# Layer 2 of a four-layer fp32 kernel: one context product a sequence, smaller steps between the score products, and a later start of the recurrence

## The chip, the cores and the metric

The kernel runs on one core of a Trainium2 chip. The metric is the device time of one execution in microseconds (us). The profile is that of another, single execution of the same program. Engines are written as the profile does: PE is TensorE (PEld its weight loads), DVE is VectorE, ACT is ScalarE, POOL is GpSimd, SP is SyncE.

## The reference

The program applies four layers to an activation x of 8 sequences of 512 positions and 128 features. Each layer does `x = x + s * silu(f)`, where s is a mixer and f a feed-forward part, both computed from the layer-normalised x. The change is inside layer 2. Its two parts are, cut to what matters:

```python
# s: _L2_attn_ref, 16 heads of 8 features, causal
qkv = ln(x) @ qkv_w + qkv_b
scores = q @ k.T / sqrt(8), future positions masked
attn = softmax(scores) @ v @ out_w + out_b
x = x + attn
ctx = attn
xs, vs = ln(x), 0
for _ in range(8):                                  # the recurrence
    u = tanh(ctx @ w_ctx + xs @ w_x + b_inl)        # ctx @ w_ctx is the same each time
    vs = vs + 0.1 * (u - xs - vs)
    xs = xs + 0.1 * vs
x = x + xs
s = x + gelu(ln(x) @ ff_w1 + ff_b1) @ ff_w2 + ff_b2
# f: _L2_ffn_ref, 128 -> 512 -> 512 -> 512 -> 128
h = silu(x @ w1 * w1_s) * (x @ w2 * w2_s)
h = gelu(h @ h1 * h1_s)
h = gelu(h @ h2 * h2_s)
f = h @ w3 * w3_s
```

## The kernel before

Everything is fp32. Layers 0, 1 and 3 stay as they are. Layer 2 works a sequence at a time; a sequence (b from 0 to 7) is a tile of 128 partitions by 512 columns, in either orientation. The 16 heads are four groups (g) of four heads, each head in a strip of 32 partitions. A *unit* is one sequence, one group and one block of 128 keys (kc from 0 to 3), so a sequence has 16 units and the layer 128. For a unit:

- `weights` computes transposed scores of the four heads into two PSUM tiles `pu` (two banks each), 512, 384, 256 or 128 columns wide as kc grows (L1390), then ACT takes the Exp (L1422) and POOL clears the future positions (L199).
- `maxima` computes, some units ahead, the scores in the other orientation (L1390) with an additive mask (L1401), also into two `pu` tiles, and DVE reduces them to the row maximum (L1404) in the tile `mpad`. `put_maxima` transposes `mpad` on PE (L1411) and adds it to the queries (L1412), in a row where the keys hold -1, so that the maximum is subtracted by the product itself.
- `sums` multiplies the weights of the unit LAG = 2 before with the values (L1435), into the bank `pf`; after the last key block the result is copied out (L120 on ACT and L122 on DVE in turn) as `oT`.

[...] two `pu` tiles of two, one `pf`, and three `pa` for all other products.

Other work is written as generators whose `yield`s cut it into steps. `begin(b)` normalises, transposes and makes queries, keys and values. `ffn(b)` computes f: four steps of w1 and w2 (L1359, L1360), then h1 and h2, each one step of sixteen products of 512 columns (L1372) with four Gelus (L1373), then w3 (L1379). `group(b, g)` transposes the sums back (L1449), divides, and after the last group makes the attention's output and the context `ctx` (L1463 to L1468). `rest(b)` normalises, runs the eight iterations of the recurrence (w_ctx L1485, w_x L1486, Tanh L1488, update L1490 to L1493), normalises again, and runs the last two products (L1509, L1515) and the way into x (L1523 to L1527).

The PE order is written out by hand: PE runs instructions just as the Python code issues them. The other engines' orders are made by a scheduler from the same program. The main loop issues, for each unit u: `weights(u)`; a step of the queue `back` (group and rest); `put_maxima` at the end of a group; a step of the queue `front` (begin and ffn of the next sequence); `maxima(u + 5)`; one more step of `back` or `front`, in turn; `sums(u - 2)`. Before the loop, the five first maxima and then all of `ffn(0)` run; after it, what is left in `back` runs alone, namely the last group and the whole `rest(7)`. A pass in what follows is one product of 128 by 128 with 512 columns, which the trace shows as two instructions.

Of the kernel before, what the change touches and what calls it, by code (L numbers as in the profile page):

```python
# [20 lines left out]
P = 128  # L21
B = 8
# [1158 lines left out]
def pack2(i):  # L1181
# [10 lines left out]
    p.add("own", one)  # L1192
    bq, bk = (strips2(b[None, n * C : (n + 1) * C]).reshape(2, P).T for n in range(2))
# [4 lines left out]
    bk[16::32] = -1.0  # L1198
    p.add("bk", bk)
# [58 lines left out]
class Layer2(BySequence):  # L1258
# [39 lines left out]
    def begin(self, b):  # L1298

        k, nc, cn, tp = self.k, self.k.nc, self.cn, self.tp  # L1300
# [13 lines left out]
        yield  # L1314
        q["xT"] = tp.tile([P, T], F32, name="xT2", bufs=1)
        k.to_features(xn, q["xT"], nt=JT)
        yield
# [4 lines left out]
        yield  # L1322
        q["qT"] = tp.tile([P, 4, T], F32, name="qT2")
        q["kT"] = tp.tile([P, 2, T], F32, name="kT2")
        for t in range(2):
# [13 lines left out]
            yield  # L1339
# [8 lines left out]
        yield  # L1348

    def ffn(self, b):  # L1350
# [5 lines left out]
        for o in range(4):  # L1356
# [8 lines left out]
            yield  # L1365
        for n in ("h1", "h2"):
            src, hA = hA, hid()
            for o in range(4):
                ps = k.pa()
                for i in range(4):  # L1370
                    c0 = i * FF2 + o * P
                    nc.tensor.matmul(ps, fn[n][:, c0 : c0 + P], src[:, i, :], start=(i == 0), stop=(i == 3))  # L1372
                nc.scalar.activation(hA[:, o, :], ps, AF.Gelu, scale=fn[n + "_s"][:, o : o + 1])  # L1373
            yield
        f = q["f"] = tp.tile([P, JT, C], F32, name="f2", bufs=3)
        ps = k.pa((P, JT, C))
        for j in range(JT):
            for i in range(4):
                nc.tensor.matmul(  # L1379
                    ps[:, j, :], hA[:, i, j * P : (j + 1) * P], fn["w3"][:, i * C : (i + 1) * C],  # L1380
                    start=(i == 0), stop=(i == 3),
                )
        nc.vector.tensor_tensor(f, ps, bc(fn["w3_s"], 1, JT), ALU.mult)
        yield
# [7 lines left out]
    def maxima(self, b, g, qt):  # L1392
        k, nc, q = self.k, self.k.nc, self.q[b]
        qT, kT = q["qT"][:, g, :], q["kT"][:, g // 2, :]
# [7 lines left out]
        for i, pu in pairs:  # L1402
            top = self.mpad[g % 2][:, qt, :].rearrange("p (i c) -> p i c", c=32)
            nc.vector.tensor_reduce(top[:, i : i + 2, 16], pu[:, :, 0:m], AX.X, ALU.max)  # L1404

    def put_maxima(self, b, g):

        k, nc, qT = self.k, self.k.nc, self.q[b]["qT"][:, g, :]
        ps = k.pa((P, JT, P))
        for t in range(JT):  # L1410
            nc.tensor.transpose(ps[:, t, :], self.mpad[g % 2][:, t, :], k.ident)  # L1411
        nc.vector.tensor_tensor(qT, qT, ps.rearrange("p a b -> p (a b)"), ALU.add)  # L1412
# [30 lines left out]
    def group(self, b, g):  # L1443
# [11 lines left out]
        yield  # L1455
# [4 lines left out]
        yield  # L1460
# [6 lines left out]
        q["ctx"] = tp.tile([P, T], F32, name="ctx2")  # L1467
# [677 lines left out]
```

## Time and profile before

| | |
|---|---|
| three runs | 3640.08, 3640.95 (median), 3649.79 us |
| profiled execution: its time, its span | 3647.2 us, 3645.5 us |
| mean granted clock of PE | 0.83 of full speed |
| layer 2, from its first maxima to its last product | 1477.5 to about 2628 us of the span |
| PE instructions of L1390, L1435, L1372, L1485, L1486 | 2048, 1024, 512, 128, 128 |
| ACT_TABLE_LOADs of layer 2 | 29 of 1.28 us each |
| PE, DVE, ACT busy over the span | 77%, 64%, 45% |

The profile names instructions by the line of the kernel, and tiles by their names in the program. A wait is put down to the engine that came last. Busy PE is modelled, so the starts of instructions tell more than their ends. The granted clock is a share of full speed; in layer 2 it is either 1.0 or 0.5 for stretches of 3.4 us.

### The profile page before, as it was taken

The page shows a single profiled execution, that of the slowest core. Times are in us where ns is not written, and L with a number is a line of the kernel's source. Part 1 is how long each engine was busy: PE and PEld are TensorE (multiplying, and loading weights), DVE is VectorE, ACT ScalarE, POOL GpSimd, SP SyncE. Part 2 cuts the span into 40 slices and gives each one's busy share as a digit, 9 for nine tenths or more (in the row PEclk, how much of TensorE's full clock was granted, in tenths as well). Part 3 has the DMA queues.
Part 4 walks back from the last instruction along what each step waited for, and adds up shares of the span by engine and source line. Part 5 has one row for each costly group of instructions (what it writes and reads, how often), then busy time and mean ns, then how long its engine had stood idle before and what let it go on. Part 6 is the DMA issues. An engine that isn't in the chain of part 4 may idle for free.

```text
span 3645.5 us, 44996 instructions
## 1 busy us (share of the span) xinstructions
PE 2815.7 (77%) x16390; PEld 1512.3 (41%) x16390; DVE 2315.1 (64%) x6346; ACT 1645.2 (45%) x3211; POOL 743.0 (20%) x845
## 2 busy tenths in 40 slices
PE   6173657512998897799999999999678789887987
PEld 4142445302444454344444444443344445444543
DVE  7989898997582334334544544444467777777775
ACT  5162546512544445233333333333245566665665
POOL 0004040400225553101101101101121222222221
PEclk9585757555789999799999999998868889888988
DMA  4003030311002222000000000000000000000000
GB/s 119 2 2 71 1 82 1 72 48 34 1 2 50 41 39 41 42 1 1 1 1 1 1 1 1 1 1 1 21 1 1 4 4 1 4 3 4 1 4 7
DMA packets 67519, 64.53 MB, mean 18 GB/s; under 512 B 5344, under 2 KB 59616, under 8 KB 66784
## 3 DMA queue, kind: packets, MB, share of 16 engines
q1 hardware_dynamic: 39264, 42.75, 3.8%
q0 software_dynamic: 19712, 14.69, 3.1%
q10 hardware_dynamic: 8320, 4.19, 0.4%
q8 instruction: 129, 2.11, 0.2%
q14 instruction: 94, 0.77, 0.1%
HBM read 43.80 MB, written 17.83 MB: 17 GB/s over the span
## 4 chain that ended last, share of the span: by engine, by line
PE 36%; DVE 17%; ACT 7%; POOL 3%; issue 2%; DMA 1%; POOLq 0%; ACTq 0%; DVEq 0%; SPq 0%
PE pa L1372 6%; PE pu L1390 6%; DVE nm L1960 4%; ACT at L1961 3%; PE pu L1957 3%; PE pf L1942 2%; DVE mpad L1404 2%; PE pf L1435 2%; PE pa L1486 1%; PE pa L1485 1%; PE pa L1870 1%; ACT at L1422 1%; PE pa L1915 1%; DVE rope L1863 1%; PE pa L1509 1%
## 5 line engine op out<-in xcount | busy, mean ns | idle before, releaser
L1961 ACT ACTIVATE at<-pu,nm 128x512 f32<-128x512 f32 x512 | 348.1, 688 | 151.6 <-DVE nm L1960 125.1
L1960 DVE TENSOR_REDUCE nm<-pu 128x1 f32<-128x512 f32 x512 | 326.8, 680 | 66.6 <-PE pu L1957 66.5
L199 POOL TENSOR_SCALAR_AFFINE_SELECT at<-at 128x512 f32<-128x512 f32 x184 | 123.3, 670 | 1004.3 <-ACT at L1422 855.9
L1404 DVE TENSOR_REDUCE mpad<-pu 128x2 f32<-128x256 f32 (+3 forms) x256 | 199.2, 818 | 168.6 <-PE pu L1401 168.6
L1422 ACT ACTIVATE at<-pu 128x1024 f32<-128x1024 f32 (+3 forms) x256 | 171.7, 702 | 285.7 <-PE pu L1390 285.5
L1078 ACT ACTIVATE at<-pu,rsqrt 128x1024 f32<-128x1024 f32 (+3 forms) x256 | 190.9, 793 | 190.1 <-PE pu L1073 164.4
L1957 PE MATMUL pu<-qT,kT 32*128 32x512 f32 x1024 | 246.4, 703 | 6.0 <-ACT at L1961 5.1
L1372 PE MATMUL pa<-hid,f 128*128 128x512 f32 x512 | 222.7, 593 | 0.0
L1390 PE MATMUL pu<-qT,kT 32*128 32x512 f32 (+3 forms) x1024 | 160.8, 516 | 56.4 <-DVE mpad L1404 42.0
L748 PE MATMUL pa<-ident,Y 128*128 128x128 f32 x32 | 7.9, 426 | 210.9 <-DVE Y L739 210.9
L1390 PE MATMUL pu<-kT,qT 32*128 32x128 f32 (+3 forms) x1024 | 151.8, 569 | 14.4 <-ACT at L1422 10.2
L1942 PE MATMUL pf<-at,va 128*32 128x512 f32 x1024 | 158.9, 698 | 1.4 <-POOL va L1935 1.4
L548 POOL DMA_INDIRECT xg<-xn_d,idx x48 | 54.9, 1143 | 496.9 <-PE pf L552 316.3
L1372 PEld LDWEIGHTS pa<-hid,f 128*128 128x128 f32 x512 | 96.6, 190 | 119.5 <-issue 118.9
L1493 DVE SCALAR_TENSOR_TENSOR X<-X,u 128x512 f32<-128x512 f32 x56 | 38.7, 691 | 159.5 <-ACT u L1488 159.5
L1073 PE MATMUL pu<-qT,kT 32*128 32x512 f32 (+3 forms) x1024 | 131.1, 518 | 5.7 <-ACT at L1078 4.7
L1390 PEld LDWEIGHTS pu<-qT,kT 32*128 32x128 f32 x1024 | 67.5, 197 | 155.5 <-DVE mpad L1404 116.3
L1016 POOL DMA_INDIRECT f_d<-ys,idx x64 | 103.6, 1619 | 138.0 <-DMA f_d<-ys,idx 86.0
L1935 POOL TENSOR_TENSOR va<-V,sm 128x32 f32<-128x32 f32 x128 | 38.8, 303 | 451.7 <-DVE sm L1934 401.5
L1957 PEld LDWEIGHTS pu<-qT,kT 32*128 32x128 f32 x1024 | 81.9, 209 | 103.2 <-ACT at L1961 65.5
L1373 ACT ACTIVATE hid<-pa,f 128x512 f32<-128x512 f32 x64 | 44.0, 688 | 172.5 <-PE pa L1372 172.5
L1083 DVE TENSOR_TENSOR at<-at,ceiling 128x512 f32<-128x512 f32 x72 | 50.2, 698 | 108.2 <-ACT at L1078 104.8
(611 smaller groups left out, 6723.3 us busy)
## 6 DMA issues: line engine op xcount, KB each, us to landing
w<-in_w_dram SPq DMA_DIRECT2D x24, 512.0 KB, 3.8
f_d<-zeros ACTq DMA_DIRECT2D x8, 512.0 KB
xn_d<-xn SPq DMA_DIRECT2D x8, 512.0 KB, 4.9
w<-in_w_dram SPq DMA_DIRECT2D x16, 256.0 KB, 2.9
w<-in_w_dram SPq DMA_DIRECT2D x24, 128.0 KB
f<-in_f_dram SPq DMA_DIRECT2D x1, 2888.0 KB, 11.8
xn<-in_x_dram SPq DMA_DIRECT2D x4, 512.0 KB, 9.3
Gt<-in_x_dram SPq DMA_DIRECT2D x4, 512.0 KB
```

The lines of the kernel that those rows point to most:

```text
L199: self.nc.gpsimd.affine_select(a, a if src is None else src, pattern, ALU.is_ge, 0.0, base=0, channel_multiplier=-1)
L1016: nc.gpsimd.indirect_dma_start(out=self.f_d, out_offset=bass.IndirectOffsetOnAxis(ap=idx[:, e, i : i + 1], axis=0), in_=ys[:, i, :], in_of ...
L1073: nc.tensor.matmul(pu[:, n, 0:m], q["kT"][r, g // 2, kc * P : kc * P + P], q["qT"][r, g, kc * P :], start=True, stop=True,)
L1078: nc.scalar.activation(at_[:, i : i + 2, 0:m], pu[:, :, 0:m], AF.Square, bias=k.rsqrt2, scale=32.0**-0.5)
L1372: nc.tensor.matmul(ps, fn[n][:, c0 : c0 + P], src[:, i, :], start=(i == 0), stop=(i == 3))
L1390: self.k.nc.tensor.matmul(pu[:, n, 0:m], a[r, c0 : c0 + P], b[r, q0 : q0 + m], start=True, stop=stop)
L1404: nc.vector.tensor_reduce(top[:, i : i + 2, 16], pu[:, :, 0:m], AX.X, ALU.max)
L1422: nc.scalar.activation(at_[:, i : i + 2, 0:m], pu[:, :, 0:m], AF.Exp, scale=8.0**-0.5)
L1942: nc.tensor.matmul(po[i * 32 : i * 32 + 32, :], va[:, kc, c0 : c0 + 32], E[:, i, :], start=(kc == 0), stop=(kc == JT - 1))
L1957: nc.tensor.matmul(pu, q["kT"][r, kc * P : (kc + 1) * P], q["qT"][r, g, :], start=True, stop=True)
L1960: nc.vector.tensor_reduce(nm[:, w], pu, AX.X, ALU.max, negate=True)
L1961: nc.scalar.activation(E[:, n, :], pu, AF.Exp, bias=nm[:, w], accum_out=sm[:, w])
```

## The change

All of it is in layer 2:

- `w_ctx @ ctx` is computed once a sequence in `group`, copied to SBUF by ACT, and added by DVE to each iteration's product before the Tanh.
- The maxima of two groups of heads lie side by side in one `mpad` (columns 16 and 17 of a strip); `put_maxima` transposes once for both and adds each to its own queries with a mask `put`. The keys hold -1 in both rows. Maxima run 9 units ahead in place of 5.
- h1 and h2 are cut into steps of two passes, with a PSUM bank `ph` of their own (one buffer), and `pa` has two buffers in place of three. w3 and ff_w2 are cut in two halves, ff_w1 too.
- Each `yield` says how many passes its step holds. The loop gives out shares of passes: one after the weights, one after the maxima; the wider the scores just issued, the larger the share. `group` goes ahead of `rest`, `rest` ahead of `front`; one step of group or rest a share, and as many of `front` as the credit allows.
- `begin(b + 1)` is put ahead of what is left of `ffn`, at the end of a sequence's second unit; the first `ffn` is woven with the first nine maxima.

The diff, cut to its core (unchanged parts of `begin`, the assertions and the constants left out):

```diff
     def ffn(self, b):
...
         for n in ("h1", "h2"):
             src, hA = hA, hid()
             for o in range(4):
-                ps = k.pa()
+                ps = k.psum("ph", (P, T))
                 for i in range(4):
+                    if i == 2:
+                        yield 2.0
                     c0 = i * FF2 + o * P
                     nc.tensor.matmul(ps, fn[n][:, c0 : c0 + P], src[:, i, :], start=(i == 0), stop=(i == 3))
                 nc.scalar.activation(hA[:, o, :], ps, AF.Gelu, scale=fn[n + "_s"][:, o : o + 1])
-            yield
+                yield 2.0
...
     def maxima(self, b, g, qt):
...
-            top = self.mpad[g % 2][:, qt, :].rearrange("p (i c) -> p i c", c=32)
-            nc.vector.tensor_reduce(top[:, i : i + 2, 16], pu[:, :, 0:m], AX.X, ALU.max)
+            top = self.mpad[g // 2][:, qt, :].rearrange("p (i c) -> p i c", c=32)
+            nc.vector.tensor_reduce(top[:, i : i + 2, 16 + g % 2], pu[:, :, 0:m], AX.X, ALU.max)
-    def put_maxima(self, b, g):
+    def put_maxima(self, b, t):
-        k, nc, qT = self.k, self.k.nc, self.q[b]["qT"][:, g, :]
+        k, nc, qT, put = self.k, self.k.nc, self.q[b]["qT"], self.cn["put"]
         ps = k.pa((P, JT, P))
-        for t in range(JT):
-            nc.tensor.transpose(ps[:, t, :], self.mpad[g % 2][:, t, :], k.ident)
-        nc.vector.tensor_tensor(qT, qT, ps.rearrange("p a b -> p (a b)"), ALU.add)
+        for qt in range(JT):
+            nc.tensor.transpose(ps[:, qt, :], self.mpad[t][:, qt, :], k.ident)
+        top = ps.rearrange("p a b -> p (a b)")
+        for v in range(2):
+            to = qT[:, 2 * t + v, :]
+            nc.vector.scalar_tensor_tensor(to, top, put[:, v : v + 1], to, ALU.mult, ALU.add)
...
     def group(self, b, g):
...
-        q["ctx"] = tp.tile([P, T], F32, name="ctx2")
-        nc.scalar.activation(q["ctx"], ps, AF.Identity, bias=self.out_bc, scale=100.0)
-        yield
+        ctx = tp.tile([P, T], F32, name="ctx2", bufs=1)
+        nc.scalar.activation(ctx, ps, AF.Identity, bias=self.out_bc, scale=100.0)
+        yield 2.25
+        ps = k.pa()
+        nc.tensor.matmul(ps, cn["w_ctx"], ctx, start=True, stop=True)
+        q["ctx"] = tp.tile([P, T], F32, name="cw2")
+        nc.scalar.copy(q["ctx"], ps)
+        yield 1.0
...
     def rest(self, b):
...
         self.layernorm(xn, h)
-        yield
-        yield
+        yield 0.0
         k.to_features(h, X[0], nt=JT, scale=self.g1[:, 0:1], bias=self.g1[:, 1:2])
-        yield
+        yield 1.25
         for it in range(ITERS):
             now, then = X[it % 2], X[1 - it % 2]
             ps = k.pa()
-            nc.tensor.matmul(ps, cn["w_ctx"], q["ctx"], start=True, stop=False)
-            nc.tensor.matmul(ps, cn["w_x"], now, start=False, stop=True)
+            nc.tensor.matmul(ps, cn["w_x"], now, start=True, stop=True)
             u = tp.tile([P, T], F32, name="u2")
-            nc.scalar.activation(u, ps, AF.Tanh, bias=cn["b_inl"], scale=0.01)
+            nc.vector.tensor_tensor(u, ps, q["ctx"], ALU.add)
+            nc.scalar.activation(u, u, AF.Tanh, bias=cn["b_inl"], scale=0.01)
...
-            yield
+            yield 1.0
...
 def layer2(k, x, A, at):
...
-        ctx.enter_context(k.banks("l2p", pu=2, pf=1, pa=3))
+        ctx.enter_context(k.banks("l2p", pu=2, pf=1, pa=2, ph=1))
...
-        AHEAD = JT + 1
-        for u in range(AHEAD):
-            L.maxima(*units[u])
-        for _ in L.ffn(0):
-            pass
-        L.put_maxima(0, 0)
         U = 4 * JT
-        front = back = iter(())
+        PAIR = 2 * JT
+        AHEAD = PAIR + 1
+        def maxima(u):
+            b, g, n = units[u]
+            L.maxima(b, g, (n - 1) % JT)
+        first = L.ffn(0)
+        for u in range(AHEAD):
+            maxima(u)
+            next(first, None)
+        L.put_maxima(0, 0)
+        for _ in first:
+            pass
+        front = groups = rest = iter(())
+        credit = 0.0
+        def fill(u, second):
+            nonlocal credit
+            wide = 1.5 - u % JT
+            share = (2.4 + 0.6 * wide, 2.4 - 0.6 * wide)[second] if u >= U else 1.8
+            share += 0.3 - 0.6 * second
+            passes = next(groups, None)
+            if passes is None:
+                passes = 0.0 if second and u % 2 == 0 else next(rest, 0.0)
+            credit = min(credit, share) + share - passes
+            while credit > 0.0:
+                passes = next(front, None)
+                if passes is None:
+                    break
+                credit -= passes
         for u in range(len(units) + LAG):
             b, n = divmod(u, U)
             if u < len(units):
                 held[u] = L.weights(*units[u])
-            next(back, None)
-            if n == 1 and b + 1 < B:
-                front = chain(L.begin(b + 1), L.ffn(b + 1))
-            if u % JT == JT - 1 and u + 1 < len(units):
-                L.put_maxima(*units[u + 1][0:2])
-            next(front, None)
+                if u % PAIR == PAIR - 1 and u + 1 < len(units):
+                    L.put_maxima(units[u + 1][0], units[u + 1][1] // 2)
+            fill(u, False)
             if u + AHEAD < len(units):
-                L.maxima(*units[u + AHEAD])
-            next(back if u % 2 else front, None)
+                maxima(u + AHEAD)
+            fill(u, True)
             if u >= LAG:
                 wb, g, kc = units[u - LAG]
                 L.sums(wb, g, kc, held.pop(u - LAG))
                 if kc == JT - 1:
-                    back = chain(L.group(wb, g), back)
+                    groups = chain(groups, L.group(wb, g))
                     if g == 3:
-                        back = chain(back, L.rest(wb))
-        for _ in back:
-            pass
+                        rest = chain(rest, L.rest(wb))
+            if n == LAG - 1 and b + 1 < B:
+                front = chain(L.begin(b + 1), front, L.ffn(b + 1))
+        for _ in chain(groups, rest):
+            next(front, None)
```

## The prediction

> **What bounds the kernel now.** I read the page first, then the busy time by stretches of layer 2, the waits of TensorE, the groups of instructions by line and form, and at last the timeline of a few places.
>
> ```profile
> PE 2815.7 (77%) x16390; PEld 1512.3 (41%) x16390; DVE 2315.1 (64%) x6346; ACT 1645.2 (45%) x3211; POOL 743.0 (20%) x845
> ```
>
> TensorE (PE) is the busiest engine. The change touches only layer 2, so I cut that layer at the first instruction of each sequence's first weights. The columns are: stretch, its length, busy PE, PEld, DVE, ACT, POOL, granted clock, DMA.
>
> ```profile
> 1477.50:1533.30 55.80, 50.85 (x179) 25.05 (x179) 15.33 (x24) 10.82 (x14) 0.00 (x0) 0.88 0.00 0
> 1533.30:1648.90 115.60, 105.79 (x598) 47.78 (x598) 39.95 (x58) 36.25 (x52) 11.41 (x17) 0.91 0.00 1
> 1648.90:1782.50 133.60, 125.16 (x686) 57.34 (x682) 60.17 (x94) 48.18 (x70) 14.57 (x20) 0.95 0.00 1
> ...
> 1919.60:2058.70 139.10, 130.74 (x719) 61.52 (x716) 65.19 (x105) 50.25 (x72) 18.31 (x23) 0.93 0.00 1
> ...
> 2472.20:2560.00 87.80, 78.85 (x498) 34.81 (x494) 43.42 (x68) 31.52 (x49) 13.18 (x18) 0.86 0.00 1
> 2560.00:2634.10 74.10, 44.32 (x170) 22.62 (x170) 28.99 (x50) 15.41 (x22) 9.58 (x12) 0.84 0.07 26
> ```
>
> These are the prologue, sequence 0, sequence 1, one of the five steady sequences (137.1 to 139.1 us), sequence 7, and the way out of sequence 7. PE is 94% busy in a steady sequence, but at clock 0.93, so about 14% of the time runs at half speed. ACT is at 36% and DVE at 47%: neither is a bound. The chain of waits over layer 2 names PE lines first, then DVE mpad L1404 (6.0%) and ACT at L1422 (3.3%). PE's own waits in this stretch are nearly all for a score bank:
>
> ```profile
> PE pu L1390 <- DVE mpad L1404: 45.9, 73, 1.7
> PE pu L1390 <- ACT at L1422: 23.2, 45, 1.4
> ```
>
> **What a sequence needs of PE.** From starts in the timeline: a pass (512 columns, two instructions) takes 0.86 us, 0.91 where the line changes; four heads' scores of 512, 384, 256, 128 columns take 1.07, 0.86, 0.65, 0.43; their sums 0.95, 0.78, 0.57, 0.36; four transposes 0.49; a mask 0.23. All work of one sequence comes to 111 us at full clock. A steady sequence takes 138, so 27 are lost. Two causes can be counted. Between weights and maxima the Exps must free the banks, between maxima and the next weights the reductions must:
>
> ```profile
> L1404 DVE TENSOR_REDUCE mpad<-pu 128x2 f32<-128x1024 f32 x64 | 75.4, 1220 | 39.8 <-PE pu L1401 39.8
> L1422 ACT ACTIVATE at<-pu 128x1024 f32<-128x1024 f32 x64 | 61.9, 1019 | 33.2 <-PE pu L1390 33.1
> ...
> L1422 ACT ACT_TABLE_LOAD x14 | 18.0, 1283 | 12.7 <-PE pu L1390 12.7
> ```
>
> Two of these in a row plus 0.2 us: 2.2 us of cover wanted after 512-wide weights, 2.6 after 512-wide maxima, less for the narrower (rows of the other forms: 808, 598, 384 and 951, 684, 418 ns). Laid along PE's order, what other work covers falls short by 15.6 us a sequence. The halved clock accounts for up to 10 more (18 us at half speed). That leaves 2: so the two causes explain the loss.
>
> **The change, part by part.** One execution carries the sum: 3647.2 us (span 3645.5), which lies 6.2 above the median of the three runs, 3640.95; my differences are put on the median.
>
> 1. *Context's product once.* L1485 goes from 16 to 2 instructions a sequence: 7 products of 0.97 us, 6.8 us of PE; its ACT copy costs 0.58 (row L120 COPY) with ACT idle. But u now needs a DVE addition of 0.69 us before the Tanh. In place of product, Tanh, update it is product, addition, Tanh, update, and the context product no longer fills PE meanwhile.
>
> 2. *Maxima in pairs of groups.* Two sets of transposes fewer, 1.0 us of PE; DVE keeps four additions (0.69 each, now with a scalar, nearest row 0.69 to 0.75), in pairs: the score of the next group waits 0.7 longer behind the pair, covered by 512-wide maxima (1.3). AHEAD 9 in place of 5 moves four maxima (3.5 us of PE) from the tail into the prologue.
>
> 3. *Steps of at most 2.5 passes, shared by width.* This is the gain aimed at. In the order of the changed kernel the 13.9-us blocks of L1372 are spread over the units, and the shortfall after maxima falls from 9.1 to 0.5 us a sequence. Shares also fall short of need: a sequence's shares come to 76.8 passes less 30.3 for groups and rest, 46.5, while begin and ffn want 52.75. Some 5 us of PE work a sequence is put off, so sequences 1 to 6 hold 99.5 us of PE work (111 less 7.8, plus 1 for more line changes, less 5), and sequence 7, which had 67, holds 89.
>
> 4. *The table loads.* Gelu now stands alone between Exps. The instruction order has 133 table loads in layer 2 where it had 29: 104 more, 13 a sequence. The trace's row says 1283 ns, so 133 us of ACT. The Trainium skill speaks against exactly this, in ScalarE: Activation LUTs, section "Table sets: the hidden batching unit": calls should be batched by table set. Its example puts about 2.7 us on a load; by that the 104 would be 281 us, an estimate from that page. The row decides: 1.28. ACT rises from 50 to 67 us a sequence, still no bound. But 67 of the loads stand before an Exp and wait with it for PE, so they lengthen the path by which banks come free from 2.2 to 3.5 us; the shortfall after weights rises from 6.5 to about 10.
>
> 5. *Banks.* ph has one buffer, pa two where it had three. A pa bank is free only after its reader; ahead of that reader on DVE stand two reductions (2.4 us), on ACT two Exps (2.0) and perhaps a load. A ph bank waits for a Gelu (0.69) behind a load (1.28). Who waits is PE, with all that is queued behind. The trace has no stall at a third pa bank; bounds: 0, and the whole queue, 3 us each.
>
> 6. *POOL and SP* keep 755 and 90 rows in both kernels' instruction orders: the causal masks, bias additions and x's addition move with their steps; no transfer is moved past another; the constants grow by two columns. I cost this at nothing: POOL, 13% busy in a steady sequence, hides it, and sums come two units after their weights, some 13 us; without that cover each mask would cost its 0.64 us (row L199).
>
> To price 3 to 5 together I followed the sixteen units of one steady sequence along the orders of PE, ACT and DVE with the durations above. PE lost: 6.2 us on Exps behind loads, 4.1 on sums' copies queued behind a Gelu or an update, 2.2 on the recurrence, 7.1 on pa banks, 2.3 on ph, 1.1 on reductions, and some 2 because PE's result reaches a reader 0.25 us after the last column. Sum 25: a steady sequence of 99.5 + 25 = 124.5 at full clock.
>
> **The clock.** The trace shows when it halves:
>
> ```profile
> 1901.10:1904.50 3.40, 1.85 (x20) 0.68 (x16) 3.37 (x8) 0.95 (x3) 1.34 (x2) 1.00 0.00 0
> 1904.50:1907.90 3.40, 3.03 (x11) 1.67 (x12) 2.27 (x5) 1.48 (x3) 1.40 (x2) 0.51 0.01 2
> ```
>
> A stretch of 3.4 us in which PE was busy 54% is followed by half clock (at 1925.0, 62%), with no gap over 1.7 us in it. The skill's TensorE: Matmul & The Clock Gate, section "Why this matters for your kernels", asks only that no gap exceed about 3 us; by that rule the changed kernel would stay at full clock, and a sequence take 124.5. By the rows, stalls of 1.4 to 2.0 us (about six places in the sequence I followed) each halve the clock for two stretches or so, 41 us; PE would lose some 14 us in them and get 5 or 6 back where later stalls vanish: 133. I take the rows.
>
> **The sum.** Sequences 1 to 6: 6 x 133 = 798 against 823.3 (the stretch rows added), -25. Sequence 0: 83 us of work, 21.5 of shortfall, 7 of bank waits, 6 of clock, 118 against 115.6, +2. Sequence 7: 89 of work, 23 of stalls (recurrence steps now stand next to each other), 6 of clock, 118 against 87.8, +30. Prologue: 3.9 us of maxima more and five ph waits of 0.95, less about 4 because PE warms up earlier, 61 against 55.8, +5. The way out: the eight iterations run alone there.
>
> ```profile
> 2590.94 1.12 PE L1486 MATMUL pa<-X,c 128*128 128x512 f32 x2
> ...
> 2592.11 0.69 ACT L1488 ACTIVATE u<-pa,c 128x512 f32<-128x512 f32 x1 [1.94 <-PE pa L1486]
> 2592.83 0.69 DVE L1493 SCALAR_TENSOR_TENSOR X<-X,u 128x512 f32<-128x512 f32 x1 [1.14 <-ACT u L1488]
> ...
> 2593.57 1.12 PE L1486 MATMUL pa<-X,c 128*128 128x512 f32 x2 [0.65 <-DVE X L1493]
> ```
>
> One takes 2.63; L1485 was hidden in it and kept PE warm. With the addition 3.36, and with PE busy a quarter of the time half clock is likely, 4.15: +11 (between 6 and 12). Total: -25 +2 +30 +5 +11 = +23 us.
>
> **Rivals.**
> *The clock holds* (the page's rule): steady sequences of 124.5, -76, the rest +48: -28, 3613 us. For it: PE work is spread evenly. Against: the rows above.
> *Only the widths' shortfall remains* (110 + 5 a sequence): sequences 1 to 6 at 690, sequence 7 at 100, sequence 0 at 106: about -120, 3520 us. For it: before, this count came within 2 us. Against: before had three pa banks and 4 Gelu visits a sequence.
> *ACT's loads lengthen every path more than I counted*, steady sequences of 142: +77, 3718 us. It decides from 129 on: there the six sequences' gain, 49, equals what prologue, sequences 0 and 7 and way out cost, 48.
> That the change doesn't do what it says: L1485's products are once a sequence in the order, so this is out.
>
> **How the numbers follow.** Forecast (133 a sequence, 3664 us): 0.54, its own spread 127.5 to 138; of it 0.08 lie within 0.3% (11 us, about what a measurement of this kernel can tell from no change). Clock holds: 0.27, of which 0.20 faster and 0.07 same. Widths only: 0.07, faster. Loads: 0.12, slower. So faster 0.27, same 0.15, slower 0.58. The range 3590 to 3722 leaves out the widths-only case and the far ends of the others.
>
> **What would show it.** Right: 133 table loads; steady sequences near 133 with clock under 0.92; PE waits on pa, ph and L1467; iterations over 3.3 us in the way out; sequence 7 near 118. Wrong: sequences under 125 with clock near 1, or DVE or ACT over 80% busy.

## The result, and the profile after

Twenty executions of each kernel: 3639.22 us after (3631.48 to 3645.72), 3645.24 before (3633.87 to 3662.48); the ratio is 0.9978, with a 95% interval of 0.9969 to 0.9988. The change made the kernel faster by 0.22%, where the forecast was 0.63% slower. The profiled execution has a span of 3638.0 us, 7.5 less than the one of before.

The page's line of the engines, first:

```profile
PE 2745.3 (75%) x16214; PEld 1453.1 (40%) x16214; DVE 2359.3 (65%) x6426; ACT 1780.1 (49%) x3323; POOL 746.6 (21%) x845
```

PE lost 70 us of busy time, and the span 7.5. So the question is where the rest went: in layer 2 PE is busy 62 us less (1058.4 to 996.7) and idle 59 us more. Here is the busy time by stretches of layer 2, cut at each sequence's first weights (length; busy PE, PEld, DVE, ACT, POOL; clock; DMA): the prologue, sequences 0, 1 and 3, sequence 7 up to its last sums, and the way out behind them.

```profile
1480.20:1536.40 56.20, 51.88 (x226) 23.64 (x225) 23.26 (x32) 10.82 (x14) 0.00 (x0) 1.00 0.00 1
1536.40:1646.90 110.50, 102.22 (x574) 43.31 (x573) 40.66 (x59) 52.44 (x65) 11.24 (x17) 0.92 0.00 1
1646.90:1782.00 135.10, 117.83 (x656) 51.62 (x652) 66.10 (x104) 61.99 (x81) 14.83 (x20) 0.92 0.00 1
...
1912.60:2043.10 130.50, 116.14 (x688) 51.63 (x684) 70.52 (x116) 61.74 (x81) 18.40 (x23) 0.96 0.00 1
...
2440.90:2556.80 115.90, 99.59 (x568) 45.01 (x564) 47.59 (x78) 65.70 (x82) 14.88 (x20) 0.96 0.00 1
2556.80:2628.50 71.70, 35.78 (x105) 15.10 (x104) 30.17 (x50) 11.54 (x17) 6.95 (x7) 0.61 0.03 8
```

The prediction ended sequence 7 of before with its last weights (87.8 us). Cut at the last sums, as here, the same two stretches of before are:

```profile
2472.40:2573.50 101.10, 88.93 (x550) 40.91 (x553) 45.35 (x70) 35.49 (x52) 14.80 (x20) 0.86 0.00 1
2573.50:2630.60 57.10, 34.03 (x119) 16.34 (x118) 24.75 (x41) 10.78 (x16) 6.80 (x7) 0.85 0.04 12
```

Against the forecast, the differences to before:

| stretch | forecast us | measured us |
|---|---|---|
| sequences 1 to 6 (794.0 against 823.3) | -25 | -29.3 |
| sequence 0 | +2 | -5.1 |
| sequence 7, to its last sums (115.9 against 101.1) | +30 | +14.8 |
| prologue, and the first projections ahead of it | +5 | +0.4, +1.9 |
| way out behind them (71.7 against 57.1) | +11 | +14.6 |
| sum over layer 2 | +23 | -2.7 |

The large movements are the forecast ones: 29 us gained in the middle, 29 given back at the end. Sequence 7 came out 15 us lower than forecast, sequence 0 seven, the middle four, the prologue with what stands ahead of it three, and the way out four higher. That carried the sum across zero.

Another 5.4 us of the 7.5 lie in layer 3, which the change does not touch and whose instructions stand in the same order in both kernels. Nearly all of it arises in one place of 36 us. Its busy time, of before and then of after, with PE's granted clock behind the busy columns:

```profile
2699.90:2735.50 35.60, 31.36 (x145) 20.75 (x144) 23.72 (x58) 14.75 (x42) 8.76 (x9) 0.67 0.00 1
```

```profile
2697.00:2733.00 36.00, 28.74 (x154) 17.54 (x150) 27.67 (x76) 18.41 (x53) 9.25 (x11) 0.82 0.00 1
```

The clock halved once more there in the execution of before (0.67), and not in that of after (0.82). Over all sixteen profiles, what follows layer 2 takes 1008 to 1010 us or, in three of them (before, and the experiments e6 and e11, which have nothing in common), 1014.9 to 1015.2. So this is a matter of the single execution. How often each kernel falls in it was not measured; of the 6 us between the medians, layer 2 accounts for 3, and the other 3 stay open.

PE's waits in layer 2 (total us, times, longest us) show what took the place of the 69 us of waits for score banks that before had:

```profile
PE pu L1404 <- ACT at L1440: 29.5, 37, 1.9
PE pa L1507 <- DVE X L1515: 23.6, 16, 2.8
PE pu L1404 <- DVE mpad L1419: 20.4, 20, 3.0
PE pa L168 <- DVE hr L1240: 14.4, 6, 5.9
PE pa L1337 <- DVE xa L172: 12.8, 4, 5.4
PE ph L1385 <- ACT hid L1386: 11.5, 12, 1.8
```

Waits for reductions (L1419) fell from 45.9 to 20.4: that is the cover by width. Waits for Exps (L1440) rose from 23.2 to 29.5. New, or far longer, are the waits for the recurrence (L1507), for h's one bank (L1385), and 12.8 us of K projections (L1337), which no step of the forecast had: with the steps of `begin` now drawn one behind the other, a K product can follow straight on the transposes that feed it. In the wait of 5.4 us at 1807.4 to 1812.9 DVE copies these transposes out (L172) only after a normalisation and two reductions of 2.35 us together.

The groups of layer 2 (busy us, mean ns of one) have the table loads that the forecast counted, 66 + 55 + 12 = 133, at 1283 ns:

```profile
L1440 ACT ACT_TABLE_LOAD x66 | 84.7, 1283 | 91.1 <-PE pu L1404 90.2
...
L1386 ACT ACT_TABLE_LOAD x55 | 70.6, 1283 | 2.0 <-PE ph L1385 1.1
...
L1531 ACT ACT_TABLE_LOAD x12 | 15.4, 1283 | 0.2
```

And the timeline of one iteration of the last recurrence (start, us, engine, line), which answers to the one shown of before:

```profile
2588.18 2.07 PE L1507 MATMUL pa<-X,c 128*128 128x512 f32 x2 [2.33 <-DVE X L1515]
2590.29 0.69 DVE L1509 TENSOR_TENSOR u<-pa,cw 128x512 f32<-128x512 f32 x1 [1.44 <-PE pa L1507]
2591.07 0.72 ACT L1510 ACTIVATE u<-u,c 128x512 f32<-128x512 f32 x1 [3.68 <-DVE u L1509]
2591.83 0.69 DVE L1515 SCALAR_TENSOR_TENSOR X<-X,u 128x512 f32<-128x512 f32 x1 [0.85 <-ACT u L1510]
...
2592.58 2.07 PE L1507 MATMUL pa<-X,c 128*128 128x512 f32 x2 [2.33 <-DVE X L1515]
```

An iteration takes 4.40 us where it took 2.63: 0.73 for the addition, and about 1 because each product takes 2.07 and not 1.12.

### The profile page after: what moved, and what is told of

It reads as the page before. It is cut to its first block, busy times and chain, and to the rows that moved or that the text cites. A ratio compares the mean times of both kernels' runs of the same rounds, so it can differ in the third digit from the quotient of the medians.

```text
span 3638.0 us, 44827 instructions
## 1 busy us (share of the span) xinstructions
PE 2745.3 (75%) x16214; PEld 1453.1 (40%) x16214; DVE 2359.3 (65%) x6426; ACT 1780.1 (49%) x3323; POOL 746.6 (21%) x845
## 4 chain that ended last, share of the span: by engine, by line
PE 31%; DVE 17%; ACT 11%; POOL 2%; issue 2%; DMA 0%; POOLq 0%; ACTq 0%; DVEq 0%; SPq 0%
PE pu L1404 6%; PE ph L1385 5%; DVE nm L2013 4%; ACT at L2014 4%; PE pu L2010 2%; PE pf L1453 2%; PE pf L1995 2%; ACT at L1440 2%; ACT L1440 1%; PE pa L1507 1%; DVE mpad L1419 1%; PE pa L1923 1%; PE pa L1968 1%; DVE rope L1916 1%; PE pu L1416 1%
## 5 line engine op out<-in xcount | busy, mean ns | idle before, releaser
L1419 DVE TENSOR_REDUCE mpad<-pu 128x2 f32<-128x1024 f32 (+3 forms) x256 | 199.1, 820 | 149.4 <-PE pu L1416 149.3
L1385 PE MATMUL ph<-hid,f 128*128 128x512 f32 x512 | 255.5, 626 | 11.6 <-ACT hid L1386 11.5
L1440 ACT ACTIVATE at<-pu 128x1024 f32<-128x1024 f32 (+3 forms) x256 | 167.2, 701 | 162.7 <-PE pu L1404 161.7
L1404 PE MATMUL pu<-kT,qT 32*128 32x512 f32 (+3 forms) x1024 | 135.4, 500 | 30.1 <-ACT at L1440 29.3
L1404 PE MATMUL pu<-qT,kT 32*128 32x512 f32 (+3 forms) x1024 | 129.8, 501 | 20.7 <-DVE mpad L1419 20.2
L1385 PEld LDWEIGHTS ph<-hid,f 128*128 128x128 f32 x512 | 94.3, 198 | 113.4 <-issue 89.6
L1073 PE MATMUL pu<-qT,kT 32*128 32x512 f32 (+3 forms) x1024 | 128.3, 507 | 6.4 <-ACT at L1078 5.5
L1440 ACT ACT_TABLE_LOAD x66 | 84.7, 1283 | 91.1 <-PE pu L1404 90.2
L2010 PEld LDWEIGHTS pu<-qT,kT 32*128 32x128 f32 x1024 | 82.2, 210 | 102.6 <-ACT at L2014 64.4
L700 DVE TENSOR_TENSOR Z<-Hs,KE 128x96 f32<-128x96 f32 x510 | 108.6, 253 | 0.9
L1097 PE MATMUL pf<-at,va 128*32 128x512 f32 (+3 forms) x1024 | 104.3, 477 | 3.9 <-issue 3.1
```

Source lines behind the costliest of these rows:

```text
L700: nc.vector.tensor_tensor(z[:, 0:3, v, :], bc(prev[:, v, :], 1, 3), bc(KE[:, o + t, 0:3, :], 2, 4), ALU.mult)
L1073: nc.tensor.matmul(pu[:, n, 0:m], q["kT"][r, g // 2, kc * P : kc * P + P], q["qT"][r, g, kc * P :], start=True, stop=True,)
L1404: self.k.nc.tensor.matmul(pu[:, n, 0:m], a[r, c0 : c0 + P], b[r, q0 : q0 + m], start=True, stop=stop)
L1419: nc.vector.tensor_reduce(top[:, i : i + 2, 16 + g % 2], pu[:, :, 0:m], AX.X, ALU.max)
L1440: nc.scalar.activation(at_[:, i : i + 2, 0:m], pu[:, :, 0:m], AF.Exp, scale=8.0**-0.5)
L2010: nc.tensor.matmul(pu, q["kT"][r, kc * P : (kc + 1) * P], q["qT"][r, g, :], start=True, stop=True)
```

## The experiments

All ratios are to the kernel before, with its own runs on the same chip. "Layer 2" is the time in the profile from its first PE instruction to its last result: 1159.4 us before, 1156.5 after. The absolute times in the expectations are on the scale of the chip that ran the batch.

| run | ratio (95% interval) | layer 2, us |
|---|---|---|
| after | 0.9978 (0.9969 to 0.9988) | 1156.5 |
| e1 context product back, sequence 7 only | 0.9942 (0.9929 to 0.9956) | 1141.1 |
| e2 one idle product an iteration, sequence 7 | 0.9968 (0.9956 to 0.9980) | 1147.9 |
| e3 three pa banks | 0.9872 (0.9857 to 0.9887) | 1115.4 |
| e4 no table loads | 0.9778 (0.9764 to 0.9791) | 1080.0 |
| e5 context product back everywhere | 1.0025 (1.0017 to 1.0033) | 1168.6 |
| e6 h uncut | 1.0471 (1.0457 to 1.0484) | 1332.7 |
| e7 before, with maxima in pairs | 0.9995 (0.9987 to 1.0003) | 1159.9 |
| e8 e1 and e3 | 0.9842 (0.9827 to 0.9856) | 1104.1 |
| e9 e3, h uncut | 1.0276 (1.0253 to 1.0299) | 1260.7 |
| e10 e8, h in steps of two products | 1.0066 (1.0052 to 1.0079) | 1188.4 |
| e11 e8, one Gelu for two products | 0.9842 (0.9822 to 0.9863) | 1103.7 |
| e12 e8, one Gelu for four products | 0.9851 (0.9830 to 0.9872) | 1105.8 |
| e13 e8, shares of 2.6 | 0.9893 (0.9878 to 0.9908) | 1115.5 |
| e14 e8, no table loads | 0.9661 (0.9648 to 0.9674) | 1039.7 |

**The last recurrence: e1 and e2.**

```
e1, in group() and rest():
+        if b == B - 1:
+            q["ctx"] = ctx
+            return
...
+            if b == B - 1:
+                nc.tensor.matmul(ps, cn["w_ctx"], q["ctx"], start=True, stop=False)
+                nc.tensor.matmul(ps, cn["w_x"], now, start=False, stop=True)
+                nc.scalar.activation(u, ps, AF.Tanh, bias=cn["b_inl"], scale=0.01)
e2, ahead of the product in rest():
+            if b == B - 1:
+                idle = k.psum("ph", (P, T))
+                nc.tensor.matmul(idle, cn["w_ctx"], q["ctx"], start=True, stop=True)
```

> The changed kernel, but in sequence 7 alone the context product goes back into the recurrence (two TensorE products an iteration, no addition on DVE, no product once a sequence). Theory A (the gain in the middle was given back in the recurrence of the last sequence, which runs alone): an iteration there goes from 4.40 us back to about 2.62, 8 x 1.78 = 14 us less, so about 3625 us. Theory B (only the DVE addition of 0.69 us costs; the half clock stays, since it was set before the iterations begin): 8 x 0.7 = 6 us less, about 3633. Theory C (other work ends the layer): within 2 us of the changed kernel.

> The changed kernel, with one more TensorE product an iteration in sequence 7, written to a bank that nobody reads; the addition on DVE stays. Theory A (an iteration's extra 1.78 us is 0.73 for the addition and 1.05 for the halved clock): clock 1.0 in the recurrence, an iteration 3.4 us, 8 us less, about 3631 us. Theory B (the clock isn't kept up by one product more): 4.4 us an iteration or up to 5.4, the product being in the way; no change or up to 8 us slower.

Busy time of the recurrence alone, in before and after (eight iterations each), e1 (four) and e2 (six):

```profile
2587.50:2609.30 21.80, 16.47 (x31) 5.38 (x29) 10.38 (x15) 5.50 (x8) 0.00 (x0) 0.93 0.00 0
```

```profile
2570.40:2605.80 35.40, 16.54 (x17) 3.98 (x17) 15.91 (x23) 5.78 (x8) 0.00 (x0) 0.50 0.00 1
```

```profile
2566.60:2577.20 10.60, 7.97 (x17) 2.75 (x17) 5.54 (x8) 2.75 (x4) 0.00 (x0) 1.00 0.00 0
```

```profile
2561.00:2581.40 20.40, 11.90 (x24) 4.06 (x24) 11.96 (x18) 4.33 (x6) 0.00 (x0) 1.00 0.00 0
```

35.4 / 8 is 4.43 us at clock 0.50; 10.6 / 4 is 2.65 at 1.00; 20.4 / 6 is 3.40 at 1.00. Theory A holds in both: layer 2 is 15.4 us shorter in e1 and 8.6 in e2. An idle product makes the iteration shorter by a microsecond, since with it the clock comes back. In before, after, e1 and e2 alike the clock falls to 0.50 just ahead of the last recurrence, where PE waits 3.1 us or more for a normalisation (L168). In before, e1 and e2 it is back at 1.00 after 6.8 us; in after it stays at 0.50 for 54.6 us. (The medians of e2 moved less, 4 us; its interval still overlaps that of after.)

**Banks: e3.**

```
-                ps = k.psum("ph", (P, T))
+                ps = k.pa()
...
-        ctx.enter_context(k.banks("l2p", pu=2, pf=1, pa=2, ph=1))
+        ctx.enter_context(k.banks("l2p", pu=2, pf=1, pa=3))
```

> The changed kernel with the banks of before: three pa banks, none for h alone. Theory A (the forecast's walk: 7.1 us a sequence lost on two pa banks, 2.3 on the one of h): seven sequences gain 5 to 9 us each, 35 to 60 us less, 3580 to 3605 us. Theory B (a half-done h product holds a pa bank through other steps, so two are left for the others as now): within 8 us of the changed kernel. Theory C (h now also waits behind the others' readers): up to 20 us slower.

Layer 2 is 41 us shorter, as theory A said. The stretches of e3, the prologue and sequences 0, 3 and 7 (this one up to the last sums; in after that is 115.9 too):

```profile
1470.50:1521.40 50.90, 50.50 (x225) 24.12 (x224) 23.25 (x33) 10.81 (x14) 0.00 (x0) 1.00 0.00 1
1521.40:1629.70 108.30, 100.00 (x577) 42.58 (x576) 40.48 (x59) 52.41 (x65) 11.20 (x17) 0.94 0.00 1
...
1885.50:2010.10 124.60, 112.22 (x684) 51.25 (x680) 69.84 (x115) 61.70 (x81) 18.09 (x23) 0.97 0.00 1
...
2394.00:2509.90 115.90, 100.11 (x572) 46.08 (x572) 47.60 (x78) 65.66 (x82) 14.84 (x20) 0.96 0.00 1
```

The gain is in the prologue (5.3) and in sequences 1 to 6 (764.3 against 794.0, so 5 each). Sequence 7 gains nothing, and sequence 0 at most 2 (it took 108.5 in e1 and e2 too, which leave it as it is).

**Table loads: e4, e14, e11, e12.** In e4 and e14 both Gelus of the layer are Tanhs, which changes what is computed.

```
-                nc.scalar.activation(hA[:, o, :], ps, AF.Gelu, scale=fn[n + "_s"][:, o : o + 1])
+                nc.scalar.activation(hA[:, o, :], ps, AF.Tanh, scale=fn[n + "_s"][:, o : o + 1])
...
-            nc.scalar.activation(hid[:, o, :], ps, AF.Gelu, bias=cn["ff_b1"][:, o : o + 1])
+            nc.scalar.activation(hid[:, o, :], ps, AF.Tanh, bias=cn["ff_b1"][:, o : o + 1])
```

> The changed kernel with Tanh in place of both Gelus of layer 2, so that all activations of the layer lie in one table set: another function is computed. It takes away all 133 table loads of the layer and leaves every step and place as it is. Theory A (the forecast's price: 6.2 us a sequence on Exps behind loads, and half of the 4.1 on sums' copies and of the 2.3 on h's bank): about 9 us a sequence, 65 us less, about 3575 us. Theory B (ACT is 47% busy, the loads lie beside other work): PE's waits for the Exp fall only by some 10 us and those for h's bank by 11, about 15 to 20 us less, 3620 us.

Layer 2 fell by 76.5 us, theory A again. In its waits, the line for the Exps went from 29.5 to

```profile
PE pu L1404 <- ACT at L1440: 2.5, 4, 1.1
```

Its stretches for sequences 0, 3 and 7:

```profile
1528.30:1631.40 103.10, 98.00 (x577) 41.29 (x576) 40.59 (x59) 33.17 (x50) 11.20 (x17) 0.93 0.00 1
...
1881.80:1999.20 117.40, 108.74 (x688) 48.68 (x684) 71.28 (x116) 43.77 (x67) 18.55 (x23) 1.00 0.00 1
...
2361.80:2473.70 111.90, 100.17 (x568) 45.46 (x564) 47.46 (x78) 40.35 (x62) 14.91 (x20) 0.92 0.00 1
```

Sequence 3 runs at full clock throughout. Named waits explain about 32 of the 76 us (27 for the Exps, 5 for h's bank), and PE's idle time in layer 2 is 35 us less in all. The other 42 are busy time. The mean clock of the layer rose from 0.921 to 0.938, which is 49 us less at half clock and so at most 25 of the 42; the rest was not traced. Sequence 7 gained 4 us, sequence 0 some 5 to 7, sequences 1 to 6 10.6 each (730.4 against 794.0).

> The best kernel so far with Tanh in place of both Gelus of layer 2, so without table loads there: another function is computed. Theory A (bank waits and load waits are separate losses): the 76 us that the loads were worth on the changed kernel come off in full, 3572 - 72 = 3500, 0.964 of the time before. Theory B (partly the same idle time: a reader late behind a load is what a bank waited for): 40 to 55 us, 0.970 to 0.973.

From e8 to e14 layer 2 falls by 64.4 us, against 76.5 from after to e4. That lies between the two theories: bank waits and load waits are separate losses for the greater part, and 12 us are common to both.

Then loads were taken away with Gelu kept and the small steps kept (e11; e12 does it with four products in place of two):

```
-                nc.scalar.activation(hA[:, o, :], ps, AF.Gelu, scale=fn[n + "_s"][:, o : o + 1])
+                nc.vector.tensor_scalar(hA[:, o, :], ps, fn[n + "_s"][:, o : o + 1], None, ALU.mult)
+                if o % 2 == 1:
+                    nc.scalar.activation(hA[:, o - 1 : o + 1, :], hA[:, o - 1 : o + 1, :], AF.Gelu)
```

> The best kernel so far, with the steps of h left as they are, but DVE copies each product out of its bank (times its scale), and one Gelu takes two products at once from SBUF: 83 loads in place of 133, the bank comes free without a load, DVE gets 8 instructions of about 0.69 us a sequence. Theory A (133 loads were worth 76 us of the layer, 0.57 us each): 50 fewer give 25 to 30 us, less 5 for DVE: 0.977 of the time before. Theory B (DVE's copies put reductions off, and the Gelu of two comes too late for the next product): no gain, 0.984 to 0.99.

> As the kernel with one Gelu for two products, but one Gelu for all four: 57 loads. Theory A (the loads go on to count): 26 loads fewer give 15 us more, 0.973. Theory B (h2 waits for a Gelu of 2.1 us or more behind a load and Exps, and Exps behind it): slower than with two, 0.98 to 0.99.

Both missed theory A; theory B held. With 83 loads, and with 57, layer 2 takes what it took with 133. Waits for an Exp in sequences 2 to 7, e8 first, then e11:

```profile
PE pu L1404 <- ACT at L1440: 18.7, 23, 1.3
```

```profile
PE pu L1406 <- ACT at L1442: 21.6, 21, 3.6
```

The groups of e11 say why:

```profile
L1442 ACT ACT_TABLE_LOAD x41 | 52.6, 1283 | 48.2 <-PE pu L1406 47.7
...
L1388 ACT ACTIVATE hid<-hid 128x1024 f32<-128x1024 f32 x32 | 33.8, 1057 | 78.1 <-DVE hid L1386 77.6
```

Fewer Exps stand behind a load (41, where 66 did), but the line ahead of such an Exp can be longer: in the longest wait, 3.6 us where it was 1.3, a load, a Gelu of 1.06 us (not 0.69) and another load stand ahead of it. In e12 the waits for Exps fall to 13.0 us, but h's own products wait 13.6 for the Gelus, which take 1.91. So here larger Gelus only moved the waits, while taking all loads away (e4, e14) removed them. DVE's copies, 48 us of work in the layer, are a further change in both that was not tested alone.

**The cut of h: e6, e9, e10.**

```
e6 (e9 the same, with "yield 8.0" and three pa banks):
-                    if i == 2:
-                        yield 2.0
...
-                yield 2.0
+            yield 4.0
e10 (on e8):
-                    if i == 2:
-                        yield 2.0
...
-                yield 2.0
+                if o % 2:
+                    yield 8.0
```

> The changed kernel with each of the two products h1 and h2 uncut: 32 matmuls and four Gelus in one step, counted as 4 passes, and no other change. Layer 2 has 57 table loads in place of 133. Theory A (the forecast's third and fourth step are both real: the cut takes 8.6 us a sequence of missing cover away and its loads cost 10): 76 loads fewer are worth 5.7 us a sequence, the cover lost costs 8.6, so 3 us a sequence slower, 20 us in all, about 3648 us. Theory B (the loads are the larger part and the blocks do little harm): up to 40 us faster, about 3590 us. Theory C (the block also puts off other steps): 3670 us.

> The changed kernel with three pa banks, none for h alone, and h1 and h2 uncut (32 matmuls and four Gelus in one step, counted as 8 passes): against the three-bank kernel (0.987 of the time before) it undoes the cut alone, without the single h bank that made TensorE wait 0.8 us at each product of the uncut kernel before it (1.047). 57 table loads in place of 133. Theory A (the cover is what counts: without h between the scores, TensorE waits for reductions and Exps and its clock halves): of the 180 us lost before, the h bank made some 50, so 1.02 to 1.04. Theory B (the loss was the h bank and what it set off): equal to the three-bank kernel or better by the 76 loads, 0.975 to 0.99.

> The best kernel so far (three pa banks, context product in the recurrence of sequence 7; 0.984 of the time before) with two whole h products and their two Gelus in a step of 8 passes: 83 loads in place of 133. Theory A (cover in small steps is worth more than loads): 50 loads are worth 29 us, blocks of 7 us leave units bare: 1.00. Theory B (a block of 7 us spoils little): 0.976.

e6 missed all its theories: 1.0471. It mixed three things: four products in a row on one h bank (43 us of waits in its trace), a count of 4 passes for a step of 16, and the cut. e9 takes the first away and keeps a wrong count (8 for 16). e10 counts right: against e8 it differs only in that two products, 7 us, come at once with their Gelus, and layer 2 is 84 us longer with 50 loads fewer. PE is idle 28 us longer there and at half clock 100 us longer, which can cost up to 50. Sequence 3 of e10 and of e9:

```profile
1917.10:2053.10 136.00, 120.76 (x681) 55.75 (x678) 70.78 (x118) 56.46 (x77) 18.01 (x23) 0.91 0.00 1
```

```profile
1937.40:2091.00 153.60, 135.43 (x696) 63.06 (x692) 71.57 (x116) 56.01 (x77) 18.19 (x23) 0.84 0.00 1
```

The clock falls with the size of the step, 0.97 (e3, e8), 0.91, 0.84 (this one with the wrong count too). Bare scores cost their wait and then the half clock that the wait brings. The waits for Exps grew most (24 to 42 us from sequence 1 to the last sums, e8 to e10); what the two Gelus that now stand together add to them was not tested apart. None of these three is the order of before, which had blocks but gave each place one step whatever its size.

**The context product: e5.** The diff is that of e1 without the condition.

> The changed kernel with the context product back in every iteration of every sequence, as before (no addition on DVE, no product once a sequence); all else as changed. The changed kernel's own time on this scale is about 3628 us, and sequence 7 alone gave 12 to 15 us when put back. Theory A (the forecast's first step: 6.8 us of TensorE a sequence saved, about 2 of it given back in waits for the addition): the seven recurrences that run beside attention cost 4 to 5 us more each, 32 in all, less the 15 of the last: about 3645 us. Theory B (the product falls into time in which TensorE waits anyway, and the addition lengthens the chain): nothing or a gain in the seven, so 3605 to 3613 us.

Against after 0.47% slower, 17 us by the medians (12 in layer 2), which is theory A's number. From sequence 1 to the last sums it takes 937.7 us against 909.9 (28 more, 4 a sequence), and the way out behind them 13 less. In sequences 1 to 6 PE's idle time is nearly the same (98 us against 94), so nearly all of the 4 us is busy time. But e5 also takes out the step that stood between the attention's output and the normalisation behind it: waits for that (L168) rose there from 5 to 36 us while those for the recurrence and the Exps fell. So the sum is measured, and not the products alone.

**Maxima in pairs: e7**, the kernel before with `put_maxima` of after and nine maxima ahead.

> The kernel before with the second part alone: maxima put into q by pairs of groups (one set of transposes and two scaled additions a pair), and nine maxima ahead in place of five. Theory A (the forecast's second step: 1.0 us of TensorE a sequence less, the four maxima moved cost nothing overall): 5 to 8 us faster. Theory B (both additions stand ahead of the next weights, 0.7 us more wait at two places a sequence, and four maxima now run in the prologue with less beside them): 0 to 8 us slower.

No difference is clear of noise (0.9987 to 1.0003): theory A fails, and of theory B only its lower end is left. Prologue and sequences 0 and 1 of e7:

```profile
1464.60:1534.20 69.60, 61.47 (x225) 30.10 (x224) 21.62 (x33) 10.82 (x14) 0.00 (x0) 0.80 0.00 0
1534.20:1653.90 119.70, 109.65 (x588) 48.99 (x588) 40.32 (x59) 36.24 (x52) 11.20 (x17) 0.86 0.00 1
1653.90:1783.80 129.90, 121.75 (x674) 54.98 (x674) 60.54 (x95) 48.20 (x70) 14.50 (x20) 0.97 0.00 1
```

The prologue loses 14 us, at clock 0.80, and sequence 0 four. Sequences 1 to 6 gain 11 (812.3 against 823.3), and what stands behind them gains 7. In after the same nine maxima have a step of the first `ffn` between any two, and the prologue runs at 1.00.

**Work put off: e13.**

```
-            share = (2.4 + 0.6 * wide, 2.4 - 0.6 * wide)[second] if u >= U else 1.8
+            share = (2.6 + 0.6 * wide, 2.6 - 0.6 * wide)[second] if u >= U else 1.8
```

> The best kernel so far (three pa banks, context product in the recurrence of sequence 7; 0.984 of the time before), with shares of 2.6 in place of 2.4 passes from sequence 1 on: the order then holds 105.5 us of TensorE work in a steady sequence in place of 100.2, and 57.5 in sequence 7 in place of 89.4. Theory A (the same work elsewhere, stalls as before): sequences 1 to 6 longer by 30 us, sequence 7 shorter by 30, within 8 us of 0.984. Theory B (work put off pays, since sequence 7 has no front of its own to cover its scores): sequence 7 shortens by 15 only, 0.988. Theory C (fuller steady sequences also have fewer stalls): 0.980.

Sequences 3 and 7 of e8, then of e13 (7 up to the last sums):

```profile
1875.20:1999.80 124.60, 112.23 (x684) 51.34 (x680) 69.83 (x115) 61.70 (x81) 18.09 (x23) 0.97 0.00 1
2383.70:2499.60 115.90, 100.09 (x570) 46.06 (x566) 47.64 (x78) 65.67 (x82) 14.85 (x20) 0.96 0.00 1
```

```profile
1896.00:2029.00 133.00, 122.44 (x700) 56.12 (x696) 70.93 (x115) 68.23 (x87) 18.30 (x23) 0.92 0.00 1
...
2428.30:2526.80 98.50, 78.06 (x498) 35.85 (x494) 43.69 (x72) 38.70 (x55) 15.08 (x20) 0.86 0.00 1
```

With 32 us of PE work taken from sequence 7 and given to 1 to 6, these grow by 26.5 us (790.8 against 764.3), and sequence 7 shrinks by 17.4. Theory B: work put off pays, because it covers the last sequence's scores. Without it sequence 7 has 32 us less to do and PE is idle there 20 us in place of 16; its clock is 0.96 with it and 0.86 without.

**Together: e8.**

> The changed kernel with three pa banks and none for h alone, and the context product in the recurrence of sequence 7. Alone these gave 12 us and 39 us on the changed kernel's 3628. If they lie in different places, as the traces put them (the last 35 us of the layer; the sequences), they add: about 3577 us. If the banks had also shortened the last recurrence's surroundings, the sum falls short: 3585 us.

0.9842: the two add within the interval (in layer 2, 52 us of 15 and 41), and this beats both kernels.

## Why the prediction was wrong

The place where it failed is the part "The sum", and there the term of sequence 7. Beyond that one, the term of sequence 0 was too large. The table gives time less the PE work that the forecast itself counted:

| us of stalls and half clock | before | forecast | after |
|---|---|---|---|
| a sequence of 1 to 6 (work 111, then 99.5) | 26 | 33.5 | 32.8 |
| sequence 0 (work 83) | 33 | 35 | 27.5 |
| sequence 7 to its last sums (work 67, then 89) | 34 | 29 | 27 |

*Sequence 7 ("89 of work, 23 of stalls ..., 6 of clock, 118 against 87.8, +30"): the failing step.* The two numbers of this subtraction do not end at the same place. Counted from the instructions of the trace at the forecast's own prices, sequence 7 of before holds 57.5 us of PE work up to its last weights and 67 up to its last sums; after holds 81 and 88. So the 67 and the 89 of the forecast run to the last sums, and so does its 118. But the 87.8 ends with the last weights; to the last sums before takes 101.1. So 13.3 us of before, whose like the 118 does cover, were left out of what it was compared with. Like for like, 118 stands against a measured 115.9, and the difference is +14.8 where +17 should have been written. Half of the error of 26 us is this. With +17 the sum would have been +10 us, 0.27%: still the wrong sign, but within what the forecast itself called the same.

That the total of 29 for stalls and clock was right within 2 us does not make its parts right: e3 shows no bank wait in this sequence, e4 puts the loads at 4 us there and not the steady 10, and e13 shows that part of the work put off is cover.

*Sequence 0 ("21.5 of shortfall, 7 of bank waits, 6 of clock", 118): a term too large.* It took 110.5, and 108.5 in e1 and e2. In e3 the banks are worth 2 us there at most, not 7; no recurrence and no group of a sequence ahead queue before the readers of pa. The rest lies in the shortfall and was not tested alone.

*Steady sequences (133 a sequence): the number right, in part by luck.* 132.3 came out, 125.9 to 138.5 in the six. But the clock is 0.94 in the mean, and the forecast had put 41 us of each sequence at half clock, which would be 0.85, and named a clock under 0.92 as its sign. At 0.94 about 16 us are at half clock, and that costs at most 8. The 8.5 that the forecast charged (14 lost, 5 or 6 got back) agrees with this in size and not in its make-up. Banks were too large and loads a little too small (steps 4 and 5 below).

*Prologue (+5).* The h bank was priced right: e3 gives back 5.3. What was too small is "less about 4 because PE warms up earlier": the clock went from 0.88 to 1.00, and e7, with the same maxima but nothing between them, lost 14 us at 0.80.

*Way out (+11): right in mechanism, low in size.* From the last sums on it took 14.6 us more. The iterations alone cost 13.6 more (21.8 to 35.4), since 4.4 us each lies above the 4.15 forecast.

*Step 1, context's product: right.* e5 measured 4 us for each sequence beside attention, 6.8 less 2.2 in the forecast.

*Step 2, maxima: right to be small.* e7 is 0, and the 1.0 us of transposes a sequence does not show in it.

*Step 3, the cut: its sign was right, its size not tested alone.* e10 puts 84 us, some 12 a sequence, on the difference between steps of 7 us and of 1.8, more than the 8.6 a sequence of the forecast would have suggested, because lost cover also halves the clock.

*Step 4, table loads: near.* 133 of them came; the walk gave them 9 us a sequence (6.2, and half of 4.1 and of 2.3), e4 10.6. But the 10.6 have the clock in them: the waits for Exps fell by 27 us in e4, 3.4 a sequence, where 6.2 were walked. That 104 more loads in themselves cost 133 us of ACT says nothing yet: e11 removed 50 and gained nothing.

*Step 5, banks: sign right, too large.* 9.4 us a sequence were walked, e3 gives 5.

*Step 6, POOL: right.* None of PE's waits in the list is for POOL.

*The clock: the rows were right against the rule, not in their amount.* The Trainium skill's page TensorE: Matmul & The Clock Gate, section "Why this matters for your kernels", asks for no gaps over about 3 us. In layer 2 of the kernel before, the clock falls to half 22 times, and in 19 of them the 3.4 us ahead of the fall hold no gap of PE over 1.7 us. In the last recurrence of after PE idles 2.33 us at a time and the clock stays at 0.50 through all eight iterations; with one product more (e2) it comes back to 1.00. The measurement decides: gaps well under 3 us do halve the clock here. By the rule the forecast would have had 124.5 us a sequence; it took 132.3.

*The chances.* The spread of the forecast, 127.5 to 138 a sequence, was put on the steady sequences alone, and these came out within 1 us of it. The 48 us of the other stretches had no spread, and there most of the error lay: of 26 us, 15 in sequence 7 and 7 in sequence 0. With 10 us either way on them, the case within 0.3% would have had more than 0.15.

## What to carry to other kernels

Before a forecast sets a counted time against a measured one, see that both end at the same instruction: here 13 us stood in one of them only, and where gains and costs nearly cancel that weighs as much as any mechanism. Walk the first and the last turn of a pipelined loop for themselves: bank waits and load waits of a steady turn carried over to them only in part, or not at all (e3, e4). A product taken out of a loop is worth having where the loop runs beside other work, and can cost where the loop runs alone and the product was free and kept the clock up: treat the last turn apart (e1: 15 us). When work is cut into smaller steps, measure the cover and the table loads each by itself, and ask how long the line ahead of the urgent instruction is, and not only how many loads there are.

## What the runs showed of the hardware that was not expected

A TensorE product whose result nobody reads made the loop around it faster: 3.40 us an iteration in place of 4.43 (e2), since the clock came back to 1.00 and stayed there. And layer 3, with the same instructions in the same order, took about 5 us more in three of sixteen profiles, through one more stretch at half clock in the one that was compared: differences of this size between single profiles are read only stretch by stretch.
